# A state-space layer with a mixture of experts: the transposed input of 15 of 16 sequences made by VectorE and DMAs

## The chip, the cores and the metric

The kernel runs on one core of a Trainium2 chip. The metric is the device time of a run in microseconds (us); lower is better. The profile is one further execution, recorded by the hardware. The engines are named as in the profile: PE (TensorE, matmuls; PEld its weight loads), DVE (VectorE), ACT (ScalarE), POOL (GpSimd), SP (SyncE, which here only issues DMAs); SPq and POOLq are the DMA issues of SP and POOL.

## The reference

Sixteen sequences of 256 tokens with 256 features, all in fp32. Both branches take the same layer-normalised input.

```python
xn = layernorm(x)                                   # (16, 256, 256)
# branch 1: selective state space, E=512, N=16, TR=128, K=4
hidden, gate = split(xn @ W_in)                     # 512 + 512 channels
hidden = silu(causal_conv4(hidden) + conv_bias)
dt, Bm, Cm = split(hidden @ W_x, [128, 16, 16])
dts = softplus(dt @ W_dt + b_dt)
state = exp(dts * A) * state + dts * Bm * hidden    # over the 256 tokens, (512, 16)
y = (sum_n(state * Cm) + hidden * D) * silu(gate)
# branch 2: 32 experts of width 96, 8 chosen for each token
w = normalised top 8 of softmax(xn @ router_w.T)
moe = sum_e w[e] * ((silu(xn @ w_gate[e]) * (xn @ w_up[e])) @ w_down[e])
out = x + y @ W_out + moe
```

## The kernel before

**Layout.** Products contract over the 256 features of x, so x is wanted with features on partitions: `xnT_b`, a tile of 128 partitions x 2 x 256 tokens. x comes in with tokens on partitions (`xt`, 128 x 2 x 256) and is normalised there. In branch 1 channels lie on partitions and time runs along the free dimension, where one scan instruction of DVE runs over the tokens.

**Steps.** Each sequence is cut into named steps, which run on one engine each. Ahead of the change: `load_x` (DMA of 256 KB), `stats` (DVE), `root` (ACT), `invert` (DVE), `norm` (ACT, L370), `turn` (PE, four 128x128 transposes into a PSUM bank `pt`, L379), `keep_turned` (ACT, a copy of 128x512 to `xnT_b`, L384). From `xnT_b` start:
- the router: `route` (PE, `pl`, L394), `largest`, `expo`, `choose` (its last instruction is a transpose of 128x64 in blocks of 32x32 on DVE, L432), `send_weights` (four DMAs of 8 KB to the DRAM tile `wd`, L441) and `spread` (six DMAs that spread the weights of eight experts over partitions, `wr`, L457);
- the experts: `gates` (`pg`) and `ups` (`pu`, both L471), `silu` (ACT, `sg`, L484), `weigh` (POOL, L490), `combine` (DVE, `h`, L494), `down` (PE, `acc`, L506), for 12 pairs of 128 columns of the hidden layer;
- the state space: `project` (PE, `ph`, L517), `conv_first` (ACT, L529), `conv_rest` (DVE, L540), `activate` (ACT, L547), `params` (PE, `px`, L555), `keep_params`, `send_params` (DMA of 32 KB to DRAM, `bcd`, L571), `widen` and `steps` (`pdt`, softplus), `inputs` (POOL, L609). Then eight groups of two states: `fetch` (DMA of 512 KB that spreads the rows of B and C over the partitions, `rep`, L618), `feed` (POOL, `bu`, L630), `decay` (ACT, `da`, L644), `scan` (DVE, L652), `read` (DVE, `pr`, L664), `collect` (POOL's DMAs that add into `y`, L669);
- the end of a sequence: `fold`, `gate` (PE, `pgate`, L697), `gate_silu`, `gated` (POOL, L713), `project_out` (PE, `po`, L723), `finish`, `store`.

**What sets the order.** A planner (`Plan`, L20 to L117) lists all steps of all sequences ahead of the build. Each step has an engine, a length, the steps that it needs, the ring slots that it takes and gives back, and a due time. On each engine the ready step with the earliest due time goes first; on ACT a step that needs no other function table counts as due `STAY` earlier; a step isn't ready before due time less `EARLY`. The instructions are then issued in that order, and each engine runs its own list in order. So a step that waits holds back what stands behind it on its engine; that holds for SP's DMAs too. Due times are a base (`ORIGIN`, `PERIOD` a sequence, `RATE` and `LEAD` for the experts) and a table entry for the kind of step (`DUE`, with `FIRST` for sequence 0 and `LAST` for sequence 15).

**Rings.** `xnT` has three slots, `rep` and `bu` three, `pr` four; PSUM has two banks each of kind `g` and `u`, used in turn by `pg`, `pu`, `ph`, `px`, `pdt`, `po` and, of kind `u`, `pt`. The tile `xt` has one slot, so the next x is loaded when this one has been turned.

Of the kernel before, what the change touches and what calls it, by code (L numbers as in the profile page):

```python
# [11 lines left out]
F32 = mybir.dt.float32  # L12
# [7 lines left out]
class Plan:  # L20
# [7 lines left out]
    SWITCH = 1.3  # L28
    HANDOVER = dict(PE=0.27, DVE=0.14, ACT=0.12, POOL=0.1, SP=0.1)
    MARGIN = dict(PE=0.4, DVE=0.1, ACT=0.1, POOL=0.1, SP=0.0)  # L30
    STAY = 8.6

    def __init__(self, rings):
        self.size = rings
# [86 lines left out]
def mamba_moe_kernel(  # L121
# [30 lines left out]
    nc = tc.nc  # L152
    P = 128
    B, L, H = x.shape
# [5 lines left out]
    HC = H // P  # L160
    EC = E // P
    SPS = L // P
# [13 lines left out]
    SPP = SLOTS // PARTS  # L176
    FAR = 1e30
    SLOWEST = 1e-26
    ORIGIN = -8.4
    PERIOD = 79.3  # L180
    RATE = 79.8

    DUE = dict(
        load_x=-120.5, stats=-16.5, root=-64.0, invert=-262.0, norm=218.5, turn=-490.0,
        keep_turned=-136.0, route=-110.0, largest=-337.5, expo=50.5, choose=-1121.5,
        send_weights=-122.5, project=-72.0, conv_first=402.5, conv_rest=236.0, activate=-361.5,
        params=-140.5, keep_params=-203.5, send_params=-258.5, widen=-105.5, steps=-57.0,
        skip=99.0, inputs=-255.0, fetch=-414.5, feed=399.0, decay=-22.0, scan=427.0, read=68.9,
        collect=-162.5, spread=41.0, gates=-37.5, ups=607.5, silu=230.0, weigh=115.0,
        combine=-69.0, down=114.0, settle=-364.0, gate=38.0, gate_silu=-13.0, fold=508.5,  # L190
        gated=598.5, project_out=-129.5, load_again=-28.5, finish=5.5,
    )
    EARLY = dict(
        load_x=169.0, load_experts=25.0, stats=37.0, turn=155.0, route=255.0, project=501.0,
    )

    FIRST = dict(
        route=248.0, largest=4.5, expo=0.5, choose=551.5, project=287.5, conv_first=-504.5,
        conv_rest=-239.5, activate=150.0, params=-457.5, keep_params=163.5, widen=6.0, steps=770.5,
        skip=-277.5, inputs=137.5, fetch=-152.0, feed=-250.0, decay=-61.0, scan=-50.5, read=-70.5,  # L200
        collect=-120.5, spread=-96.0, gates=-48.0, ups=-216.5, silu=-173.5, weigh=271.5,
        combine=239.0, down=-66.5,
    )

    LAST = dict(
        fetch=-293.5, feed=1.0, decay=252.5, scan=589.0, read=109.5, collect=-95.0, spread=0.5,
        gates=198.5, ups=131.0, silu=192.0, weigh=-110.0, combine=538.5, down=189.5, settle=2.5,
        gate=7.5, gate_silu=223.0, fold=-22.5, gated=238.5, project_out=-415.5, finish=519.5,
    )
    LEAD = -29.6  # L210
    TOPK = 8
    EPS = 1e-5

    xf = x.rearrange("b l h -> (b l) h")
# [3 lines left out]
    p1 = ctx.enter_context(tc.tile_pool(name="p1", bufs=1))  # L218
    sb = ctx.enter_context(tc.tile_pool(name="sb", bufs=1))
    ps = ctx.enter_context(tc.tile_pool(name="ps", bufs=1, space=PSUM))  # L220
    dram = ctx.enter_context(tc.tile_pool(name="dram", bufs=3, space=DRAM))

    RINGS = dict(
        sk=1, xt=1, mv=1, st=1, std=1, xnT=3, nmax=1, rest=1, dt=1, hs=2, dts=2, y0=2, y1=2,
        rep=3, bu=3, pr=4, da=AHEAD, g=2, u=2, acc=1, wr=2, sg=3, h=2, gs=2, o=1,
    )
    taken = defaultdict(int)
# [8 lines left out]
    live = {}  # L236
# [129 lines left out]
    def norm(b):  # L366
        xt = live["xt", b]
        rstd, nmr = live.pop(("st", b))
        for s in range(SPS):
            nc.scalar.activation(  # L370
                xt[:, s, :], xt[:, s, :], AF.Identity, bias=nmr[:, s, :], scale=rstd[:, s, :]
            )

    def turn(b):
        xn = live.pop(("xt", b))
# [371 lines left out]
    b = 0  # L747
    MM = 0.432
    KB = 1 / 280

    def add(kind, key, engine, length, due, *args, early=None, **kw):
        fn = kw.pop("fn", None) or steps_of[kind]
        if early is None:
            early = EARLY.get(kind, 1e9)
        due += DUE.get(kind, 0.0) + (FIRST.get(kind, 0.0) if b == 0 else 0.0)
        due += LAST.get(kind, 0.0) if b == B - 1 else 0.0
        plan.add((kind, *key), engine, length, due, fn, *args, early=early, **kw)

    steps_of = dict(
        load_x=load_x, stats=stats, root=root, invert=invert, norm=norm, turn=turn,  # L760
        keep_turned=keep_turned, route=route, largest=largest, expo=expo, choose=choose,
        project=project, conv_first=conv_first, conv_rest=conv_rest, activate=activate,
        params=params, keep_params=keep_params, widen=widen, steps=steps, skip=skip, inputs=inputs,
        fetch=fetch, spread=spread, gates=gates, ups=expand, silu=silu, combine=combine,
        weigh=weigh, down=down, settle=settle, gate=gate, gate_silu=gate_silu, gated=gated,
        project_out=project_out, load_again=load_again, finish=finish, store=store, feed=feed,
        add_skip=add_skip, fold=fold, send_params=send_params, send_weights=send_weights, collect=collect, decay=decay, scan=scan, read=read,
        turn_router=turn_router, keep_router=keep_router, warm=warm, grow=grow, shrink=shrink, load_router=load_router, load_in=load_in,
        load_steps=load_steps, load_out=load_out, load_experts=load_experts,
    )  # L770
# [14 lines left out]
    for b in range(B):  # L785
        t = ORIGIN + PERIOD * b
        last = [] if b else [("load_in", 0)]
        x = ("x", b)
        add("load_x", (b,), "SP", 256 * KB, t if b else -210.0, b, takes=[("xt", x)],
            needs=[("turn", b - 1)] if b else [], lands=11.0 if b else 3.5)  # L790
        add("stats", (b,), "DVE", 0.9, t, b, needs=[("load_x", b)],
            takes=[("mv", ("mv", b)), ("st", ("st", b)), ("std", ("rs", b))], gives=[("st", b)])
# [3 lines left out]
            gives=[("mv", b)])  # L796
        add("norm", (b,), "ACT", 1.09, t, b, needs=[("invert", b)],
            gives=[("rs", b)])
        xT = ("xnT", b)
        add("turn", (b,), "PE", 1.0, t, b, needs=[("norm", b)], gives=[x],  # L800
            takes=[("u", ("pt", b)), ("xnT", xT)])
        add("keep_turned", (b,), "ACT", 0.6, t, b, needs=[("turn", b)],
            gives=[("pt", b)])
        add("route", (b,), "PE", 0.9, t if b else t + 30.0, b, needs=[("keep_turned", b), ("keep_router",)],
            takes=[("g", ("pl", b)), ("nmax", ("nmax", b)), ("rest", ("rest", b))], gives=[xT])
        add("largest", (b,), "DVE", 0.25, t, b, needs=[("route", b)])
# [31 lines left out]
        add("inputs", (b,), "POOL", 2.5, t, b, needs=[("steps", b, 0), ("steps", b, 1),  # L838
            ("params", b)] + [("skip", b, c) for c in range(EC)])
        for g in range(GROUPS):  # L840
            at = t + PERIOD / GROUPS * g
            add("fetch", (b, g), "SP", 512 * KB, at, b, g, needs=[("send_params", b)],
                takes=[("rep", ("rep", b, g))], lands=5.5, early=14.0)

        for r in range(UNITS):
            k = UNITS * b + r
            g, u = divmod(r, PAIRED)
            at = t + PERIOD / UNITS * r
            add("feed", (k,), "POOL", 2.31, at, k, needs=[("fetch", b, g), ("inputs", b)],
                takes=[("bu", ("bu", k))], gives=[hs])  # L850
            for j in range(CPU):
# [27 lines left out]
        for i in range(PAIRS // BATCH):  # L879
            at = e + RATE * BATCH / PAIRS * i  # L880
            qs = range(BATCH * i, BATCH * (i + 1))
            for q in qs:
                part = 2 * q // CPG
                add("ups", (b, q), "PE", 4 * MM, at, b, q, "u", gives=[xT], takes=[("u", ("u", b, q))],
                    needs=[("keep_turned", b)] + ([] if b else [("load_experts", part, "u")]))
                add("weigh", (b, q), "POOL", 1.23, at, b, q, gives=[("wr", b, part)],
                    needs=[("silu", b, i), ("spread", b, part)])
                add("combine", (b, q), "DVE", 0.6, at, b, q,
                    needs=[("weigh", b, q), ("ups", b, q)],
                    takes=[("h", ("h", b, q))], gives=[("u", b, q), ("sg", b, q)])  # L890
                add("down", (b, q), "PE", 4 * MM, at, b, q, gives=[("h", b, q)],
                    needs=[("combine", b, q)] + ([("down", b, q - 1)] if q else [])
# [10 lines left out]
            gives=[("acc", b)])  # L903
# [57 lines left out]
```

## Time and profile before

| | |
|---|---|
| median of 3 runs (lowest to highest) | 1326.89 us (1322.99 to 1330.68) |
| the profiled execution, its own time | 1322.61 us |
| its span, first to last instruction | 1320.8 us |
| granted clock of PE, mean | 0.996 |
| turn: PE transposes / ACT copies | x64, 11.2 us busy / x16, 9.4 us busy |
| ACT table loads for decay / silu (L484) / steps | x148 / x81 / x29, 1283 ns each |
| POOL bu, L630 | x256, 715.5 us busy, 68.2 us idle before it |
| SPq rep waiting for DVE pr | 342.3 us, 79 times |

Busy time is what an instruction group took on its engine; idle before it is time in which the engine had nothing to do until that instruction could start, with the instruction that released it. The time of a run is the span and 1.8 us around it. Waits of SP are often no loss: the queue stands ready until a buffer is free. PE's records are pipelined, so a matmul shown with 381 ns starts about 216 ns after the one ahead of it; what a group costs on PE is read from the starts of its neighbours.

### The profile page before, as it was taken

How to read it: one execution, taken by the hardware profiler on the slowest of the kernel's cores; microseconds unless marked ns; L12 is line 12 of the kernel's file. 1: busy time of each engine (PE TensorE's matmuls, PEld its weight loads, DVE VectorE, ACT ScalarE, POOL GpSimd, SP SyncE). 2: the span in 40 equal slices, each digit the busy share in tenths (PEclk: the TensorE clock that was granted, in tenths of full speed). 3: DMA queues.
4: the chain of work that ended last, by engine and by line, in shares of the span. 5: the costliest groups of instructions: out<-in, count | busy, mean ns of one | idle time of the engine just before them, and what ended most of it. 6: DMA issues, size and time to landing. Idle time of an engine off the chain costs nothing.

```text
span 1320.8 us, 18891 instructions
## 1 busy us (share of the span) xinstructions
PE 1290.6 (98%) x5968; PEld 1108.5 (84%) x5968; DVE 1178.9 (89%) x1735; ACT 1129.6 (86%) x1895; POOL 1184.6 (90%) x803
## 2 busy tenths in 40 slices
PE   8999999999999999999999999999999999999998
PEld 6878888878888887888888888888888888888887
DVE  3688999899989999989999898998989899899986
ACT  5888798888888988899898998989899898988873
POOL 0789899989998998998999999998999989898995
PEclk9999999999999999999999999999999999999999
DMA  9998898898988999999899998999889899998994
GB/s 252 238 254 190 193 212 208 198 210 192 216 187 178 217 219 203 199 197 216 189 216 199 219 204 185 217 198 216 199 194 216 191 205 198 208 205 192 196 222 93
DMA packets 174035, 268.79 MB, mean 204 GB/s; under 512 B 37840, under 2 KB 112112, under 8 KB 173936
## 3 DMA queue, kind: packets, MB, share of 16 engines
q0 software_dynamic: 40672, 124.80, 50.4%
q1 hardware_dynamic: 130624, 142.75, 39.9%
q8 instruction: 47, 0.77, 0.2%
q10 hardware_dynamic: 2640, 0.05, 0.1%
q14 instruction: 52, 0.43, 0.1%
HBM read 137.51 MB, written 5.24 MB: 108 GB/s over the span
## 4 chain that ended last, share of the span: by engine, by line
PE 56%; DVE 13%; POOL 10%; DMA 8%; issue 7%; ACT 5%; SPq 0%; ACTq 0%; POOLq 0%; DVEq 0%
PE pu L471 14%; PE acc L506 14%; PE pg L471 13%; DVE da L652 6%; DMA rep<-bcd 5%; POOL bu L630 4%; PE px L555 4%; DVE pr L664 3%; PE po L723 3%; POOL sg L490 3%; PE ph L517 3%; PE pgate L697 2%; ACT da L644 2%; POOL y L669 2%; PE pdt L578 2%
## 5 line engine op out<-in xcount | busy, mean ns | idle before, releaser
L630 POOL TENSOR_TENSOR bu<-rep,hs 128x1024 f32<-128x1024 f32 x256 | 715.5, 2947 | 68.2 <-DVE da L652 44.2
L652 DVE TENSOR_TENSOR_SCAN da<-da,bu 128x512 f32<-128x512 f32 x512 | 608.2, 1216 | 40.1 <-ACT da L644 36.2
L644 ACT ACTIVATE da<-dts,a_sb 128x256 f32<-128x256 f32 x1024 | 468.9, 473 | 88.2 <-DVE pr L664 64.7
L471 PE MATMUL pu<-xnT,wu_sb 128*128 128x256 f32 x1536 | 361.7, 381 | 9.5 <-DVE h L494 8.6
L506 PE MATMUL acc<-wd_sb,h 128*128 128x256 f32 x1536 | 363.2, 379 | 0.9 <-DVE h L494 0.8
L471 PE MATMUL pg<-xnT,wg_sb 128*128 128x256 f32 x1536 | 349.9, 381 | 4.0 <-ACT sg L484 3.2
L490 POOL TENSOR_TENSOR sg<-sg,wr 128x512 f32<-128x512 f32 x192 | 318.2, 1971 | 34.8 <-ACT sg L484 34.4
L471 PEld LDWEIGHTS pu<-xnT,wu_sb 128*128 128x128 f32 x1536 | 291.3, 191 | 52.3 <-DVE h L494 11.7
L471 PEld LDWEIGHTS pg<-xnT,wg_sb 128*128 128x128 f32 x1536 | 292.4, 191 | 47.0 <-ACT sg L484 5.3
L669 POOL DMA_DIRECT2D y<-pr x222 | 319.8, 1446 | 9.7 <-DVE pr L664 3.7
L506 PEld LDWEIGHTS acc<-wd_sb,h 128*128 128x128 f32 x1536 | 291.2, 190 | 41.3 <-DVE h L494 2.0
L664 DVE TENSOR_TENSOR pr<-da,rep 128x512 f32<-128x512 f32 x448 | 294.2, 677 | 3.4 <-DMA y<-pr 1.6
L644 ACT ACT_TABLE_LOAD x148 | 189.9, 1283 | 2.6
L494 DVE TENSOR_TENSOR h<-pu,sg 128x512 f32<-128x512 f32 x192 | 131.1, 683 | 52.0 <-POOL sg L490 25.3
L484 ACT ACTIVATE sg<-pg 128x512 f32<-128x512 f32 x192 | 105.3, 594 | 8.3 <-PE pg L471 5.5
L484 ACT ACT_TABLE_LOAD x81 | 103.9, 1283 | 3.0 <-PE pg L471 1.6
L540 DVE SCALAR_TENSOR_TENSOR hs<-ph,small,hs 128x255 f32<-128x255 f32 (+2 forms) x192 | 76.1, 471 | 0.0
L713 POOL TENSOR_TENSOR y<-y,gs 128x512 f32<-128x512 f32 x30 | 74.3, 2953 | 0.1
L555 PE MATMUL px<-hs,wx_sb 128*32 128x256 f32 (+1 forms) x256 | 62.8, 393 | 3.0 <-ACT sg L484 3.0
L723 PE MATMUL po<-wout_sb,y 128*128 128x256 f32 x256 | 60.9, 381 | 4.1 <-POOL y L713 3.1
L517 PE MATMUL ph<-xnT,win_sb 128*128 128x256 f32 x256 | 64.3, 397 | 0.0
L688 POOL TENSOR_TENSOR y<-y 128x512 f32<-128x512 f32 x32 | 63.9, 2399 | 0.1
(65 smaller groups left out, 868.5 us busy)
## 6 DMA issues: line engine op xcount, KB each, us to landing
y<-pr POOLq DMA_DIRECT2D x222, 512.0 KB, 7.4
rep<-bcd SPq DMA_DIRECT2D x128, 512.0 KB, 6.1
wr<-wd SPq DMA_DIRECT2D x128, 192.0 KB, 5.4
wr<-wd SPq DMA_DIRECT2D x128, 128.0 KB, 5.5
wr<-wd SPq DMA_DIRECT2D x128, 64.0 KB, 5.3
y<-sk POOLq DMA_DIRECT2D x32, 256.0 KB, 5.9
xt<-L_attn_input_states_dram SPq DMA_DIRECT2D x16, 256.0 KB, 5.7
o<-L_attn_input_states_dram SPq DMA_DIRECT2D x16, 256.0 KB, 6.8
```

The lines of the kernel that those rows point to most:

```text
L471: nc.tensor.matmul(p[:, j, :], w[:, hc, ts(c, P)], xs[:, hc, :], start=(hc == 0), stop=(hc == HC - 1),)
L484: nc.scalar.activation(sg, live.pop(("g", b, q)), AF.Silu)
L490: nc.gpsimd.tensor_mul(sg, sg, wr[:, r : r + 2, :])
L494: nc.vector.tensor_mul(h, live.pop(("u", b, q)), live.pop(("sg", b, q)))
L506: nc.tensor.matmul(acc[:, s, :], h[:, j, ts(s, P)], wd_sb[:, c, :], start=(c == 0 and s == 0), stop=(c == FC - 1), skip_group_check=True,)
L517: nc.tensor.matmul(ph[:, j, :], win_sb[:, hc, ts(2 * q + j, P)], xs[:, hc, :], start=(hc == 0), stop=(hc == HC - 1),)
L555: nc.tensor.matmul(p, w[:, c, :], hs[:, c, :], start=(c == 0), stop=(c == EC - 1))
L630: nc.gpsimd.tensor_mul(bu, live["rep", b, g][:, 0:1].to_broadcast([P, CPU, NG, L]), live["hs", b][:, ts(u, CPU), :].unsqueeze(2).to_broadc ...
L644: nc.scalar.activation(da[:, i, :], dts[:, c, :], AF.Exp, scale=a_sb[:, c, n : n + 1])
L652: nc.vector.tensor_tensor_scan(flat, flat, live["bu", k][:, j].rearrange("p n l -> p (n l)"), 0.0, op0=ALU.mult, op1=ALU.add,)
L664: nc.vector.tensor_mul(live["pr", k][:, j], live.pop(("da", m)), live["rep", b, g][:, 1])
L669: nc.gpsimd.dma_start(live["y", b, u].rearrange("p c n l -> p (c n l)"), live.pop(("pr", k)).rearrange("p c n l -> p (c n l)"), accum_op=A ...
```

## The change

For sequences 1 to 15 the step `turn` moves from PE to DVE: one instruction transposes each 32x32 block of `xt` within itself, into a new tile `xb` (one slot). The blocks are then put in their places by DMAs on SP: `send_x` writes them to a DRAM tile `xd` of 256 features x 256 tokens, in eight DMAs of 32 partitions x 8 x 32 elements (32 KB each, runs of 32 floats), and `keep_turned` reads `xd` back as `xnT_b` in one DMA of 256 KB. Sequence 0 keeps the transposes of PE and the copy of ACT. All constants of the planner's due times change, a table for sequence 1 is added, and `STAY` goes from 8.6 to 16.9. What is computed is the same.

```diff
-    STAY = 8.6
+    STAY = 16.9
...
-    ORIGIN = -8.4
+    ORIGIN = -7.2
     PERIOD = 79.3
-    RATE = 79.8
+    RATE = 79.0
...
     EARLY = dict(
-        load_x=169.0, load_experts=25.0, stats=37.0, turn=155.0, route=255.0, project=501.0,
+        load_x=153.0, load_experts=21.0, stats=37.0, turn=7.0, send_x=91.0, route=363.0,
+        project=463.0,
     )
...
-    LEAD = -29.6
+    LEAD = -39.2
     TOPK = 8
+    TB = 32
...
-        sk=1, xt=1, mv=1, st=1, std=1, xnT=3, nmax=1, rest=1, dt=1, hs=2, dts=2, y0=2, y1=2,
+        sk=1, xt=1, xb=1, mv=1, st=1, std=1, xnT=3, nmax=1, rest=1, dt=1, hs=2, dts=2, y0=2, y1=2,
...
+    def flip(b):
+        xn = live.pop(("xt", b))
+        xb = p1.tile([P, SPS, H], F32, tag="xb", name=f"xb_{b}")
+        nc.vector.transpose(
+            xb.rearrange("p s h -> p (s h)"), xn.rearrange("p s h -> p (s h)")
+        )
+        live["xb", b] = xb
+
+    def send_x(b):
+        xb = live.pop(("xb", b)).rearrange("p s (g t) -> p s g t", t=TB)
+        xd = dram.tile([H, L], F32, tag="xd", name=f"xd_{b}")
+        for q in range(P // TB):
+            for s in range(SPS):
+                nc.sync.dma_start(
+                    xd.rearrange("(g h) (s q t) -> s q h g t", h=TB, s=SPS, t=TB)[s, q],
+                    xb[ts(q, TB), s],
+                )
+        live["xd", b] = xd
+
+    def fetch_x(b):
+        xs = take(sb, "xnT", [P, HC, L], f"xnT_{b}")
+        nc.sync.dma_start(xs, live.pop(("xd", b)).rearrange("(c p) l -> p c l", p=P))
+        live["xnT", b] = xs
...
+        due += SECOND.get(kind, 0.0) if b == 1 else 0.0
...
-        add("turn", (b,), "PE", 1.0, t, b, needs=[("norm", b)], gives=[x],
-            takes=[("u", ("pt", b)), ("xnT", xT)])
-        add("keep_turned", (b,), "ACT", 0.6, t, b, needs=[("turn", b)],
-            gives=[("pt", b)])
+        if b == 0:
+            add("turn", (b,), "PE", 1.0, t, b, needs=[("norm", b)], gives=[x],
+                takes=[("u", ("pt", b)), ("xnT", xT)])
+            add("keep_turned", (b,), "ACT", 0.6, t, b, needs=[("turn", b)],
+                gives=[("pt", b)])
+        else:
+            add("turn", (b,), "DVE", 0.6, t, b, fn=flip, needs=[("norm", b)], gives=[x],
+                takes=[("xb", ("xb", b))])
+            add("send_x", (b,), "SP", 3.4, t, b, needs=[("turn", b)], gives=[("xb", b)], lands=6.0)
+            add("keep_turned", (b,), "SP", 256 * KB, t, b, fn=fetch_x, needs=[("send_x", b)],
+                takes=[("xnT", xT)], lands=6.0)
```

Left out are the new values of `DUE`, `FIRST` and `LAST`, of which nearly all change, and the new table `SECOND` with 44 entries (from -192.0 to 224.0).

More of the change, by code (lines that the diff above doesn't have):

```diff
@@ L178, in mamba_moe_kernel @@
     SLOWEST = 1e-26
-    ORIGIN = -8.4
+    ORIGIN = -7.2
     PERIOD = 79.3
-    RATE = 79.8
+    RATE = 79.0
     DUE = dict(
[L184 to L191, printed above, removed]
+        load_x=-72.5, stats=-15.5, root=-34.5, invert=-76.5, norm=313.5, turn=-598.5,
+        keep_turned=-111.5, route=-118.5, largest=-237.5, expo=87.0, choose=-1192.0,
+        send_weights=-223.5, project=-27.0, conv_first=583.5, conv_rest=131.0, activate=-475.5,
+        params=-116.5, keep_params=-304.5, send_params=-109.0, widen=-214.5, steps=-60.5,
+        skip=-24.0, inputs=-315.5, fetch=-278.0, feed=405.5, decay=-23.0, scan=431.5, read=69.4,
+        collect=-148.5, spread=-13.5, gates=-8.0, ups=707.0, silu=266.0, weigh=215.0,
+        combine=-242.5, down=338.5, settle=-523.5, gate=45.0, gate_silu=-13.0, fold=572.0,
+        gated=595.0, project_out=-2.0, load_again=-46.5, finish=-43.0,
@@ L192, in mamba_moe_kernel @@
     )
     EARLY = dict(
-        load_x=169.0, load_experts=25.0, stats=37.0, turn=155.0, route=255.0, project=501.0,
+        load_x=153.0, load_experts=21.0, stats=37.0, turn=7.0, send_x=91.0, route=363.0,
+        project=463.0,
     )
     FIRST = dict(
-        route=248.0, largest=4.5, expo=0.5, choose=551.5, project=287.5, conv_first=-504.5,
-        conv_rest=-239.5, activate=150.0, params=-457.5, keep_params=163.5, widen=6.0, steps=770.5,
-        skip=-277.5, inputs=137.5, fetch=-152.0, feed=-250.0, decay=-61.0, scan=-50.5, read=-70.5,
@@ L201, in mamba_moe_kernel @@
-        collect=-120.5, spread=-96.0, gates=-48.0, ups=-216.5, silu=-173.5, weigh=271.5,
-        combine=239.0, down=-66.5,
+        route=214.5, largest=-39.0, expo=113.0, choose=475.5, project=260.5, conv_first=-707.0,
+        conv_rest=-293.5, activate=296.0, params=-346.5, keep_params=261.5, widen=23.5,
+        steps=847.0, skip=-301.0, inputs=142.0, fetch=-175.5, feed=-16.5, decay=-38.5, scan=167.5,
+        read=-22.5, collect=-252.0, spread=-144.5, gates=-65.5, ups=-212.0, silu=-128.0,
@@ new lines, in mamba_moe_kernel @@
+        weigh=293.5, combine=226.5, down=-220.5,
+    )
+    SECOND = dict(
+        load_x=-192.0, stats=-103.5, root=-105.5, invert=224.0, norm=-87.5, turn=-135.0,
+        keep_turned=123.0, route=-11.5, largest=-54.0, expo=-82.5, choose=57.5,
+        send_weights=-107.0, project=-25.5, conv_first=-31.5, conv_rest=108.5, activate=-23.5,
+        params=-3.5, keep_params=39.5, send_params=220.5, widen=-95.5, steps=149.0, skip=-20.0,
+        inputs=212.5, fetch=-6.0, feed=-21.5, decay=-94.5, scan=41.5, read=29.5, collect=79.0,
+        spread=-67.0, gates=9.0, ups=-10.0, silu=51.5, weigh=14.0, combine=87.5, down=-21.0,
+        settle=96.5, gate=3.5, gate_silu=167.5, fold=-40.5, gated=91.0, project_out=46.0,
+        load_again=-41.5, finish=190.0,
@@ L203, in mamba_moe_kernel @@
     )
     LAST = dict(
-        fetch=-293.5, feed=1.0, decay=252.5, scan=589.0, read=109.5, collect=-95.0, spread=0.5,
-        gates=198.5, ups=131.0, silu=192.0, weigh=-110.0, combine=538.5, down=189.5, settle=2.5,
-        gate=7.5, gate_silu=223.0, fold=-22.5, gated=238.5, project_out=-415.5, finish=519.5,
+        fetch=-267.0, feed=61.5, decay=327.5, scan=428.0, read=-123.0, collect=-218.0, spread=16.5,
+        gates=123.0, ups=381.5, silu=249.0, weigh=-155.0, combine=676.0, down=153.5, settle=-109.0,
@@ L209, in mamba_moe_kernel @@
+        gate=-57.5, gate_silu=105.0, fold=154.0, gated=126.5, project_out=-437.0, finish=566.5,
     )
-    LEAD = -29.6
+    LEAD = -39.2
     TOPK = 8
+    TB = 32
     EPS = 1e-5
@@ L372, in norm @@
             )
+    def flip(b):
[13 more added lines that the diff above has]
+                    xb[ts(q, TB), s],
+                )
+        live["xd", b] = xd
[3 more added lines that the diff above has]
+        live["xnT", b] = xs
     def turn(b):
@@ L766, in mamba_moe_kernel @@
         project_out=project_out, load_again=load_again, finish=finish, store=store, feed=feed,
-        add_skip=add_skip, fold=fold, send_params=send_params, send_weights=send_weights, collect=collect, decay=decay, scan=scan, read=read,
+        add_skip=add_skip, fold=fold, send_params=send_params, send_x=send_x, send_weights=send_weights, collect=collect, decay=decay, scan=scan, read=read,
         turn_router=turn_router, keep_router=keep_router, warm=warm, grow=grow, shrink=shrink, load_router=load_router, load_in=load_in,
```

## The prediction

> **What bounds the kernel now.** I read first the page's busy shares, then the windows of 80 us, then the chain of waits, then the queue of SP.
>
> ```profile
> span 1320.8 us, 18891 instructions
> PE 1290.6 (98%) x5968; PEld 1108.5 (84%) x5968; DVE 1178.9 (89%) x1735; ACT 1129.6 (86%) x1895; POOL 1184.6 (90%) x803
> ...
> q0 software_dynamic: 40672, 124.80, 50.4%
> q1 hardware_dynamic: 130624, 142.75, 39.9%
> ```
>
> Four engines and the DMAs are all near full; PE is the fullest, with 1320.8 - 1290.6 = 30.2 us idle. Where those lie, the windows tell (length, busy time and instructions of PE, PEld, DVE, ACT, POOL, then clock, DMA share, GB/s):
>
> ```profile
> 240.00:320.00 80.00, 77.59 (x363) 66.69 (x362) 75.81 (x108) 69.03 (x115) 75.27 (x52) 1.00 0.91 199
> 720.00:800.00 80.00, 80.00 (x376) 69.46 (x376) 73.60 (x111) 72.21 (x120) 74.97 (x52) 1.00 0.91 204
> 800.00:880.00 80.00, 80.00 (x376) 69.45 (x376) 73.27 (x109) 72.19 (x121) 74.80 (x51) 1.00 0.93 203
> ```
>
> From about 640 to 1120 us PE never stops; from 160 to 640 us it loses 12.2 us (the six windows there have 77.46, 77.59, 77.23, 80.00, 77.33, 78.24 busy), 2.0 us for each sequence. The chain of waits says what one stretch of PE costs (start, length, what):
>
> ```profile
> 767.79 1.73 PE acc L506 x8
> 769.51 0.44 PE pt L379 x4
> 769.95 1.73 PE pu L471 x8
> 771.68 3.45 PE pgate L697 x16
> ```
>
> The pieces abut: 767.79 + 1.73 is 769.52, where the four transposes start, and 0.44 us later comes the next product. The next pgate of the chain starts at 851.03: one sequence costs 79.35 us, all of it PE. So here time off PE is time off the end, until another engine takes over; DVE has 80 - 73.3 = 6.7 us left in 80, POOL 5.0, ACT 7.8.
>
> A rule of the Trainium skill would read this otherwise. "Perfetto Trace Analysis" (Identifying the Most-Contended Engine) says that matmul busy time misjudges how near PE is to its limit, and wants LDWEIGHTS busy time. Here that is 69.46 of 80, which would leave 10.5 us free, and taking transposes away would bring nothing. But the chain shows instructions that abut, with no release between them; I go by the chain.
>
> **What goes.** Of 16 sequences, 15 lose four transposes on PE: 15 x 0.44 = **6.6 us**. PE's waits for them go too: for the normalised x 2.2 us in all, of which 1.4 belong to sequence 0, which keeps its transposes, so 0.8; and 1.0 for the copy that empties their bank (pu waiting for ACT xnT). Together **1.8 us**. ACT loses 15 copies of 0.59 us (8.8 us), and by the order of its instructions 8 of 308 table switches at 1.283 us (10.3 us): it is not on the chain in the steady stretch, so I count nothing for that.
>
> **What DVE gets.** One transpose of 128x512, which the trace doesn't show. The nearest row is that of the small one (L432):
>
> ```profile
> L432 DVE STREAM_TRANSPOSE wT<-rest 128x64 f32<-128x64 f32 x16 | 3.9, 245 | 0.5
> ```
>
> Two other DVE rows give a slope: a product of 128x64 takes 224 ns (L429), one of 128x512 677 ns (L664), so 1.0 ns per element. 245 + 448 x 1.0 gives 0.70 us; the upper end is eight of the small ones, 1.96 us. I take 0.7, as only the stream grows. Both ends fit in DVE's 6.7 us. Without that cover it would be 15 x 0.7 = 10.5 us.
>
> **What the DMAs get.** Per sequence eight writes of 32 KB in runs of 32 floats (128 B), that is 2,048 packets, and one read of 256 KB in 256 packets of 1 KB. Here a rule speaks against the change: "VectorE: DVE Perf Modes" (The three transpose paths) warns that a plain DMA that transposes by strides is 19 times slower than the crossbar's 1.309 us for 128x128 in bf16. By that rule (an estimate from that page) 256 KB, eight such blocks, would take 8 x 19 x 1.309 = 199 us per sequence, more than twice the period, and the kernel would take some 15 x (199 - 79) = 1,800 us more. But the elements were turned before, inside blocks of 32, and the DMA moves whole runs. The trace has just such a transfer: wd<-wT writes rows of 32 floats into rows of DRAM 1 KB apart.
>
> ```profile
> wd<-wT SPq DMA_DIRECT2D x64, 8.0 KB, 4.2
> rep<-bcd SPq DMA_DIRECT2D x128, 512.0 KB, 6.1
> bcd<-bc SPq DMA_DIRECT2D x16, 32.0 KB, 4.5
> ```
>
> The 4,096 packets of 128 B took 14.8 ns each in the trace's packet records, those of 1 KB on the same queue 55.6 ns. So 2,048 x 14.8 / 16 engines = 1.9 us, and 256 x 55.6 / 16 = 0.9: **2.8 us of DMA time per sequence** on some 73 (0.92 of 79.35). The other end is the mean of all packets of q1 (39.9% of 16 x 1320.8 us over 130,624 packets: 64.6 ns), 8.3 us for the writes. I take the row of like packets. The share isn't a ceiling at 1: it adds packets of both queues that overlap, and stretches of 1 us at 1.2 occur (919 to 920 us). Cover: rep, the only DMA on the chain, has room, as follows.
>
> **What SP gets, and who queues behind.** Eight issues of 0.6 us (median of wd<-wT) are 4.8 us, and the read must wait for the last write to land (4.2 to 4.5 us by the last rows). In the new order of SP the eight stand (but for sequences 1 and 2) between rep_1 and rep_4 of the sequence before; behind them stand a rep, the wr of that quarter, and the next x. In all 15 a rep stands between the writes and the read, so the writes mostly land during a wait that SP has anyway (it waits 342 us for DVE pr in all). How late may a rep be? In the steady stretch rep_0 is issued at 900.26, lands about 6.1 later, and its first feed on POOL starts at 912.96: 6.6 us to spare; for rep_1 (908.81, feed 922.27) 7.4; for rep_2 (917.50, feed 934.73) 11. The 4.8 us are covered. Uncovered, a late rep stops POOL's bu, and behind it DVE's scans and POOL's sg, for which h and then PE wait.
>
> The new path for one x is 0.7 + 4.8 + 4.2 + 5.7 (xt's landing as the row for the read) = 15.4 us, against 0.44 + 0.59 before. In the steady stretch of before the transposes end at 928.5 and route starts at 944.0: 15.5 us, so at the old places this would just do. But the new order has the writes behind rep_1 or rep_2, and the read of most sequences right behind rep_2 or rep_3. In the times of before, rep_3 goes out at 928.5, so xnT would land near 935, 9 us ahead of route. So x comes in time: cost nothing; only in sequence 15, where the read follows rep_4 (937.64 + 5.7 = 943.3), is there no room.
>
> **What moves.** All due times are new, so the order changes everywhere. Two things I can weigh. In the order before, sequences 7 to 12 repeat nearly the same list, the one that keeps PE full; after, hardly two agree. From the gates to the product with their h there lie at least 28 matmuls (12.1 us) in those sequences before, 20 to 24 in sequences 6, 7, 10, 11 and 12 after. And from ph to px, for which convolution and silu took 6.2 us in the trace (791.4 to 797.6), there are 28 matmuls before, 12 (5.2 us) in sequence 2 after: 1.0 us of wait there. In the first 100 us sequence 1's projection goes behind 192 matmuls and transposes in place of 84, so that PE has experts' work where it waited 8.2 us (12 to 130 us). I count these against each other as nothing, with 12 us to the worse (2.0 us of wait in each of the six full sequences as in the earlier ones) and 6 us to the better (half of the 12.2 us).
>
> **Sum.** The profiled run took 1322.6 us (span 1320.8 and 1.8 around it). 1322.6 - 6.6 - 1.8 = 1314.2. The median of the three runs shown is 1326.9, 4.3 above it; the same saving from there gives **1318.5**.
>
> **The rivals.** A measurement of this kernel can tell about 0.5%, 6.6 us, from no change: faster is below 1320.3, slower above 1333.5.
> - *As summed*, 1318.5, its own range 1313 to 1324: chance 0.45. For: the abutting pieces. Against: the gain is just the size of what can be told.
> - *The new order also fills earlier waits*: 6 us more, 1312.5. Chance 0.18. For: 8.2 us of waits near the start, and a bank less in use.
> - *The uneven order brings waits back* in the full stretch: 1318.5 + 12 = 1330.5. Chance 0.22. For: the shorter distances. Against: every other engine has 5 us or more to spare in each sequence, and can catch up.
> - *Slower: SP holds rep back.* If the writes land like the slowest wd (7.9 us) while SP stands at the read, a rep comes 4.8 + 7.9 = 12.7 us late. Beyond 6.6 us POOL's bu starves, 6.1 us, and beyond POOL's spare 79.35 - 74.9 = 4.4 the sequence gets longer: 1.7 x 15 = 25 us, 1344. From a lateness of 11 us on it decides. Against: the rep between. Chance 0.15.
>
> That the change doesn't do what it says is out: the four transposes are gone from PE's order in 15 sequences.
>
> Range 1308 to 1335: it leaves out most of the last rival and the lower edge of the second. Faster: two thirds of the first case and the second, 0.48; slower: the last and a quarter of the third, 0.21; same 0.31.
>
> **What would show it.** Right: pgate to pgate near 78.9 us in a stretch with PE at 80.00 of 80; PE busy near 1284; the transpose at 0.7 us; the writes landing in 4 to 5 us with 15 ns packets; no wait of POOL bu for rep beyond 1,000 us. Wrong: PE below 79 of 80 in windows after 640 us (by h: the order; by pl or ph for xnT: the path of x), bu waiting for rep, or packets of 128 B much slower than 15 ns, with the DMA share at 1 and rep landing late.

## The result, and the profile after

The changed kernel takes **1368.66 us** in the median of four runs (1363.49 to 1375.12), the kernel before 1324.94 beside it: a ratio of 1.0335 (95%: 1.0305 to 1.0365). It is slower, by 44 us; 1318.5 was forecast, so the forecast is 50 us off. The profiled execution took 1363.49 us.

The page of the changed kernel, its span, busy shares and DMA queues:

```profile
span 1361.6 us, 18968 instructions
...
PE 1300.4 (96%) x5908; PEld 1113.5 (82%) x5908; DVE 1195.5 (88%) x1750; ACT 1113.4 (82%) x1872; POOL 1184.1 (87%) x803
...
q0 software_dynamic: 40672, 124.80, 48.9%
q1 hardware_dynamic: 167344, 150.62, 41.6%
```

PE has the 60 matmuls less that were forecast, and is still busy for 9.8 us more. Idle is 1361.6 - 1300.4 = 61.2 us, where it was 30.2. These two parts, 31.0 and 9.8, are the whole growth of the span (40.8 us). The windows of 80 us that stood in the prediction show where (length, busy time and instructions of PE, PEld, DVE, ACT, POOL, then clock, DMA share, GB/s):

```profile
240.00:320.00 80.00, 76.83 (x355) 65.79 (x355) 75.41 (x109) 65.48 (x112) 72.57 (x49) 1.00 0.88 195
...
720.00:800.00 80.00, 76.10 (x347) 65.48 (x347) 69.82 (x106) 66.94 (x114) 69.70 (x49) 0.98 0.89 197
800.00:880.00 80.00, 77.11 (x353) 66.14 (x352) 70.22 (x107) 67.90 (x114) 72.14 (x49) 0.98 0.93 205
```

PE, at 80.00 of 80 from 720 to 880 us before, now pauses there, and does 347 and 353 matmuls instead of 376 in such a window. No other engine has become full: DVE and POOL do less in these windows than before. In the two later ones the clock is 0.98 in place of 1.00. So no engine got more work than it can do; the work seems to come at the wrong times, and the experiments look for the reason.

The new pieces themselves have the prices that were worked out. The view of DMA issues (KB each, median us from issue to landing) and groups of DVE (count, busy us, mean ns, idle before it; the row of L361 is from the kernel before):

```profile
rep<-bcd SPq DMA_DIRECT2D x128, 512.0 KB, 6.7
...
xd<-xb SPq DMA_DIRECT2D x120, 32.0 KB, 5.3
xnT<-xd SPq DMA_DIRECT2D x15, 256.0 KB, 7.1
...
wd<-wT SPq DMA_DIRECT2D x64, 8.0 KB, 4.8
```

```profile
L361 DVE SCALAR_TENSOR_TENSOR nmr<-mv,rstd 128x2 f32<-128x2 f32 x16 | 21.8, 1360 | 0.6
...
L374 DVE SCALAR_TENSOR_TENSOR nmr<-mv,rstd 128x2 f32<-128x2 f32 x16 | 32.0, 1999 | 0.6
...
L703 DVE TENSOR_TENSOR pr<-da,rep 128x512 f32<-128x512 f32 x448 | 293.6, 675 | 1.3
...
L392 DVE STREAM_TRANSPOSE xb<-xt 128x512 f32<-128x512 f32 x15 | 10.3, 688 | 3.8 <-ACT xt L383 3.8
```

The transpose takes 688 ns (forecast 0.70 us), and the packets of 128 B take 14.9 ns each in the packet records (forecast 14.8). But rep lands in 6.7 us instead of 6.1, and an instruction that the change doesn't touch, nmr, a product of two columns, takes 1999 ns in the mean instead of 1360. What stands behind these two is told with the experiments.

**One stall, followed from end to end.** The worst of the windows is 160 to 240 us, with PE at 71.74 of 80 (77.46 before). The chain of waits leads through `221.36 8.56 DMA rep<-bcd`; the timeline, here taken from four engines (start, length, what, and idle time before it with its releaser), shows both ends of it:

```profile
207.43 8.16 SPq L402 DMA_DIRECT2D xd<-xb  x8
215.69 5.03 SPq L496 DMA_DIRECT2D wr<-wd  x6
220.81 0.42 SPq L253 DMA_DIRECT2D xt<-L_attn_input_states_dram  x1
221.36 0.39 SPq L657 DMA_DIRECT2D rep<-bcd  x1
...
230.09 2.33 POOL L669 TENSOR_TENSOR bu<-rep,hs 128x1024 f32<-128x1024 f32 x1 [8.17 <-DMA rep<-bcd]
...
234.91 0.69 DVE L533 TENSOR_TENSOR h<-pu,sg 128x512 f32<-128x512 f32 x1 [7.34 <-POOL sg L529]
...
235.66 3.78 PE L545 MATMUL acc<-wd_sb,h 128*128 128x256 f32 x8 [5.12 <-DVE h L533]
...
241.99 1.89 PE L545 MATMUL acc<-wd_sb,h 128*128 128x256 f32 x8
```

SP issues without a pause from 207.43 to 221.36: the eight writes hold it for 8.2 us, the six wr for 5.0, then x, and only then rep. rep lands 8.56 us later. Its buffer had been free since 215.49, when DVE's last read of it ended, so the queue held this rep for 5.9 us. POOL has stood for 8.17 us for it; behind bu stands POOL's sg, for which DVE's h waits, and for h PE waits 5.12 us. PE pays once more: the eight matmuls after the pause take 3.78 us, where the same eight take 1.89 a little later. That is half the clock: the trace's clock records have 0.50 from 232.67 on, for 6.83 us.

### The profile page after: what moved, and what is told of

It reads as the page before. It is cut to its first block, busy times and chain, and to the rows that moved or that the text cites. A ratio compares the mean times of both kernels' runs of the same rounds, so it can differ in the third digit from the quotient of the medians.

```text
span 1361.6 us, 18968 instructions
## 1 busy us (share of the span) xinstructions
PE 1300.4 (96%) x5908; PEld 1113.5 (82%) x5908; DVE 1195.5 (88%) x1750; ACT 1113.4 (82%) x1872; POOL 1184.1 (87%) x803
## 4 chain that ended last, share of the span: by engine, by line
PE 49%; DVE 12%; POOL 11%; ACT 10%; DMA 9%; issue 8%; SPq 1%; ACTq 0%; POOLq 0%; DVEq 0%
PE acc L545 12%; PE pg L510 11%; PE pu L510 11%; DVE da L691 5%; POOL bu L669 4%; PE px L594 3%; PE po L762 3%; ACT da L683 3%; POOL sg L529 3%; DVE pr L703 3%; PE ph L556 3%; DMA rep<-bcd 3%; PE pgate L736 2%; DMA wr<-wd 2%; DMA xnT<-xd 2%
## 5 line engine op out<-in xcount | busy, mean ns | idle before, releaser
L669 POOL TENSOR_TENSOR bu<-rep,hs 128x1024 f32<-128x1024 f32 x256 | 703.9, 2878 | 90.9 <-DVE da L691 46.2
L545 PE MATMUL acc<-wd_sb,h 128*128 128x256 f32 x1536 | 369.9, 384 | 14.4 <-DVE h L533 14.4
L545 PEld LDWEIGHTS acc<-wd_sb,h 128*128 128x128 f32 x1536 | 295.5, 193 | 58.3 <-DVE h L533 16.2
L708 POOL DMA_DIRECT2D y<-pr x222 | 292.9, 1327 | 27.6 <-DVE pr L703 11.4
L523 ACT ACTIVATE sg<-pg 128x512 f32<-128x512 f32 x192 | 105.2, 594 | 15.9 <-DVE h L533 8.9
L556 PE MATMUL ph<-xnT,win_sb 128*128 128x256 f32 x256 | 67.7, 412 | 0.0
L762 PEld LDWEIGHTS po<-wout_sb,y 128*128 128x128 f32 x256 | 49.3, 195 | 16.4 <-POOL y L752 8.2
## 6 DMA issues: line engine op xcount, KB each, us to landing
wr<-wd SPq DMA_DIRECT2D x128, 192.0 KB, 5.3
```

The source lines that it names most:

```text
L523: nc.scalar.activation(sg, live.pop(("g", b, q)), AF.Silu)
L545: nc.tensor.matmul(acc[:, s, :], h[:, j, ts(s, P)], wd_sb[:, c, :], start=(c == 0 and s == 0), stop=(c == FC - 1), skip_group_check=True,)
L556: nc.tensor.matmul(ph[:, j, :], win_sb[:, hc, ts(2 * q + j, P)], xs[:, hc, :], start=(hc == 0), stop=(hc == HC - 1),)
L669: nc.gpsimd.tensor_mul(bu, live["rep", b, g][:, 0:1].to_broadcast([P, CPU, NG, L]), live["hs", b][:, ts(u, CPU), :].unsqueeze(2).to_broadc ...
L708: nc.gpsimd.dma_start(live["y", b, u].rearrange("p c n l -> p (c n l)"), live.pop(("pr", k)).rearrange("p c n l -> p (c n l)"), accum_op=A ...
L762: nc.tensor.matmul(po[:, s, :], y[:, j, 0, ts(s, P)], wout_sb[:, c, :], start=(c == 0 and s == 0), stop=(c == EC - 1), skip_group_check=True,)
```

## The experiments

Three causes were to be told apart: the **writes** (SP held, packets, a late x), the **order** (all due times new), and **nmr** on DVE. Each time is the median beside runs of the kernel before, with the ratio to it and its 95% interval.

**Order and way crossed.** The first run takes the new due times, but leaves the turn on PE for all sequences except sequence 1, which keeps the new way. The second takes the old due times and the new way of x.

```diff
-        if b == 0:
+        if b != 1:
             add("turn", (b,), "PE", 1.0, t, b, needs=[("norm", b)], gives=[x],
```

> The changed kernel's due times, but sequences 2 to 15 are turned by PE and copied by ACT as before (sequence 1 keeps the DMA way, since without it the planner finds no order with these due times). If the order that the new due times make is what costs (order theory): 1350 to 1370 us, with half-clock stretches of PE as in the changed kernel. If the way of x by DVE, DRAM and SP costs (DMA theory): 1320 to 1330.

> The old due times and STAY, with sequences 1 to 15 turned by DVE and DMAs. Order theory: the old due times keep PE full in the second half, 1315 to 1330 us. DMA theory: 1350 us or more, with PE waiting for xnT and POOL for rep. If any due times have to be tuned for the way of x, this one is the slowest of all, over 1370, and neither theory alone holds.

Measured: 1377.83 us, 1.0391 (1.0361 to 1.0421), and 1393.07 us, 1.0512 (1.0472 to 1.0552). Both mixtures are slower than the kernel before, and the second is slower than the changed one; the first is so by 9 us, but its interval just overlaps. So neither theory holds alone: the new due times are slow without most of the DMAs too, and the new way with the old due times costs more (67 us) than with its own (44). The two runs can't split the loss into parts, as each builds an order of its own.

**Taking the writes away.** The order stays that of the changed kernel, instruction for instruction but for the eight writes. The read takes x itself, so the data are not turned, and what is computed from them isn't the layer.

```diff
-        for q in range(P // TB):
-            for s in range(SPS):
-                nc.sync.dma_start(
...
-        nc.sync.dma_start(xs, live.pop(("xd", b)).rearrange("(c p) l -> p c l", p=P))
+        live.pop(("xd", b))
+        nc.sync.dma_start(xs, xf[ts(b, L), :].rearrange("(c p) h -> p c h", p=P))
```

> The changed kernel's order of steps, but the eight writes of each x to DRAM are left out and the read of 256 KB takes the input x itself from DRAM, so xnT doesn't hold the turned x and the output isn't the reference's. DMA theory: SP is no longer held for 6 to 8 us a sequence and no read waits for writes, so 1320 to 1330 us. Order theory: 1350 to 1365.

Measured: 1340.53 us, 1.012 (1.0089 to 1.0152). This run splits the error: **1368.7 - 1340.5 = 28 us for the eight writes, and 1340.5 - 1318.5 = 22 us for the rest**, which is the new order with DVE's transposes and the read of 256 KB left in. The page and the waits (total us, times, longest) of this run:

```profile
span 1338.4 us, 18799 instructions
```

```profile
POOL bu L664 <- DMA rep<-bcd: 15.9, 11, 2.7
...
PE acc L540 <- DVE h L528: 4.8, 2, 3.9
```

In the changed kernel the same two rows are, with one more, and then POOL's row in the kernel before:

```profile
POOL bu L669 <- DMA rep<-bcd: 28.9, 15, 8.2
...
PE acc L545 <- DVE h L533: 14.4, 7, 5.1
...
PE pl L433 <- DMA xnT<-xd: 8.1, 3, 3.9
```

```profile
POOL bu L630 <- DMA rep<-bcd: 16.1, 11, 3.1
```

So POOL's long waits for rep, and two thirds of the time that acc waits for h, come with the writes; without them POOL waits for rep as in the kernel before. The third row, the router's product waiting for the new x, looked like another cost.

**A late x, packets, or the queue of SP?** One run keeps the writes, but reads x from the input, so that the read need not wait for their landing. A second also cuts each write to one eighth of its packets. In both, xnT isn't the turned x.

```diff
-        nc.sync.dma_start(xs, live.pop(("xd", b)).rearrange("(c p) l -> p c l", p=P))
+        nc.sync.dma_start(xs, xf[ts(b, L), :].rearrange("(c p) h -> p c h", p=P))
...
-                    xd.rearrange("(g h) (s q t) -> s q h g t", h=TB, s=SPS, t=TB)[s, q],
-                    xb[ts(q, TB), s],
+                    xd.rearrange("(g h) (s q t) -> s q h g t", h=TB, s=SPS, t=TB)[s, q][:, 0:1],
+                    xb[ts(q, TB), s][:, 0:1],
```

> The changed kernel with its eight writes, but the read takes the input x from DRAM and so waits for no write (xnT then doesn't hold the turned x). Leaving the writes out together with that wait gave 1340.5 us, 28 less than the changed kernel. If it is the late x (the wait of the read for the writes, and of route for the read): near 1343. If it is what the writes do to SP and to the other DMAs: 1360 or more.

> As the last, with an eighth of each write: 32 packets in place of 256, the same eight issues on SP (xnT doesn't hold the turned x). If SP's time and its waits for free places cost: as the last run within 3 us. If the packets cost (1.9 us of all DMA engines a sequence): nearer to 1340.

Measured: 1368.5 us, 1.032 (1.0288 to 1.0352), and 1353.88 us, 1.0213 (1.0185 to 1.0242). Freeing the read changes nothing. But this run doesn't settle what a late x costs: the read still stands behind the writes on SP, and pl still waits 9.7 us for it. So one more run issued that read, of x itself as before, from ACT's queue:

```diff
-        nc.sync.dma_start(xs, xf[ts(b, L), :].rearrange("(c p) h -> p c h", p=P))
+        nc.scalar.dma_start(xs, xf[ts(b, L), :].rearrange("(c p) h -> p c h", p=P))
```

> The changed kernel with its eight writes on SP, but the read takes the input x from DRAM and is issued by ACT, so it stands behind no write and waits for none (xnT doesn't hold the turned x). In the earlier run with a free read PE still waited 9.7 us for xnT, since the read stood behind the writes on SP. If the late x is what the hold on SP costs: 1345 to 1355. If the hold costs by rep and wr: 1360 to 1370.

Measured: 1370.83 us, 1.0343 (1.0305 to 1.0382). Now pl waits only 1.2 us for xnT, and the time is that of the changed kernel. That speaks against a late x as the main cost, but doesn't rule it out: with the read on its queue ACT lets pl wait 5.7 us for a decay (1.7 in the changed kernel), and POOL waits longer for rep. The rows of the three runs (read freed, fewer packets, read on ACT):

```profile
POOL bu L670 <- DMA rep<-bcd: 26.5, 13, 8.8
```

```profile
POOL bu L670 <- DMA rep<-bcd: 13.5, 12, 2.7
...
PE acc L546 <- DVE h L534: 9.8, 6, 3.5
...
PE pl L434 <- DMA xnT<-L_attn_input_states_dram: 9.2, 3, 3.6
```

```profile
POOL bu L670 <- DMA rep<-bcd: 37.3, 14, 10.0
...
PE pl L434 <- ACT da L684: 5.7, 2, 2.9
```

From the first to the second run seven eighths of the packets go, and 14.6 us with them; POOL's long waits for rep go too. From there to no writes at all it is another 13.4 us (1353.9 - 1340.5), for eight small DMAs that still hold SP. These 13.4 us don't come by way of rep, for which POOL waits no longer than in the run without writes (13.5 and 15.9 us). PE waits longer for h (9.8 against 4.8) and for xnT (9.2 against 3.0); what the hold delays on the way there was not separated, and a late x may be part of it.

From the first issue to the end of the eighth the small writes take 6.5 us in the mean of 15 sequences, and those of the changed kernel 7.5 (5.2 to 11.6), where 4.8 was forecast. Why it is more than eight times a single issue (median 456 ns), the waits of SP's queue in the changed kernel tell only in part:

```profile
SPq L402 <- DMA wr<-wd: 7.7, 11, 2.2
...
SPq L402 <- DMA rep<-bcd: 6.0, 7, 2.1
```

The writes don't read wr or rep; they wait for earlier DMAs on the same queue to land. But the two rows are 13.7 us in 15 sequences, 0.9 of the 7.5 us. Of the rest most lies in the issues themselves: eight take 6.1 us in the mean, and a single one up to 4.68. What draws these out isn't shown.

**Fewer, larger writes.** Four writes of 64 KB with the same packets:

```diff
-            for s in range(SPS):
-                nc.sync.dma_start(
-                    xd.rearrange("(g h) (s q t) -> s q h g t", h=TB, s=SPS, t=TB)[s, q],
-                    xb[ts(q, TB), s],
-                )
+            nc.sync.dma_start(
+                xd.rearrange("(g h) (s q t) -> q h s g t", h=TB, s=SPS, t=TB)[q],
+                xb[ts(q, TB)],
+            )
```

> The changed kernel with four writes of 64 KB in place of eight of 32 KB, the same 2,048 packets of 128 B. If the number of issues holds SP: about half of what an eighth of the packets left (13 us), so 1360 to 1363. If only the packets count: 1366 to 1370.

Measured: 1362.11 us, 1.0281 (1.0252 to 1.031). SP is held 5.3 us in the mean, and the median is 6.6 us lower; the intervals of the ratios overlap by a hair, so the direction is likely and the size uncertain. POOL's wait for rep is longer here than in the changed kernel, so that wait alone doesn't set the time:

```profile
POOL bu L668 <- DMA rep<-bcd: 35.1, 16, 7.0
```

**The writes on another queue.** If SP's hold is the cost, ACT might issue the writes:

```diff
-                nc.sync.dma_start(
+                nc.scalar.dma_start(
```

> The changed kernel with its eight writes issued by ACT in place of SP, all else equal. Packets stay, SP's hold (7.5 us a sequence in the profile) goes, ACT gets it, with some 10 us to spare in 80. If the hold on SP is the larger part of the 28 us: 1345 to 1352. If the packets are: 1358 to 1368. If ACT can't bear the hold in the middle of its exponentials: over 1370.

> The changed kernel with both the writes issued by ACT and nmr made by ACT. If the two parts add to what the moved nmr alone brought (1354): 1335 to 1345; if ACT's hold makes up for it: 1354 or more.

Measured: 1466.25 us, 1.1075 (1.1039 to 1.1111); and with the edit of nmr below on top 1455.81 us, 1.0976 (1.0939 to 1.1013). POOL's wait for rep falls to 9.9 us, as it should, but the hold has only moved:

```profile
ACT da L683 <- DMA xd<-xb: 46.0, 5, 15.4
ACT L683 <- DMA xd<-xb: 41.7, 5, 10.7
```

The decays don't read xd: between the two ends of such a wait ACT does nothing but issue the eight writes (510.89 to 517.39 us in one case). Meanwhile it owes decays to DVE, which waits 145.5 us for them, where it was 31.0 in the changed kernel. SP was the better place: it has time between its issues.

**The small instruction on DVE.** In the changed kernel nmr (-mean x rstd, 128x2) once takes 7.57 us. What POOL does in that time (timelines of DVE, POOL and PE):

```profile
524.97 7.57 DVE L374 SCALAR_TENSOR_TENSOR nmr<-mv,rstd 128x2 f32<-128x2 f32 x1
532.46 1.27 DVE L703 TENSOR_TENSOR pr<-da,rep 128x512 f32<-128x512 f32 x2
...
524.23 2.63 POOL L669 TENSOR_TENSOR bu<-rep,hs 128x1024 f32<-128x1024 f32 x1
526.53 1.17 POOL L708 DMA_DIRECT2D y<-pr  x1
527.14 2.94 POOL L669 TENSOR_TENSOR bu<-rep,hs 128x1024 f32<-128x1024 f32 x1
529.45 3.06 POOL L529 TENSOR_TENSOR sg<-sg,wr 128x512 f32<-128x512 f32 x2
...
534.39 3.78 PE L545 MATMUL acc<-wd_sb,h 128*128 128x256 f32 x8 [3.85 <-DVE h L533]
```

nmr ends when POOL's row of products ends (529.45 + 3.06 = 532.51), DVE does nothing else meanwhile, and PE waits 3.85 us for the h behind it. The Trainium skill, "SBUF — State Buffer" (SBUF: two separate sides), says that VectorE and GpSimd share a pair of ports, which one instruction holds alone until it ends, and names a DVE operation with two SBUF inputs as one that needs it. The trace agrees only in part. All eight uses of nmr above 1 us in the changed kernel ended within 0.1 us of the end of a POOL instruction. But the longest outlasts several of them, and the products pr, which have two SBUF inputs as well, don't wait: 303 of the 448 began and ended within a tensor instruction of POOL, and none took more than 0.69 us. So what sets nmr apart isn't shown. The next test can show what nmr costs on DVE, not that the ports hold it. It gives the product to ACT, as three small instructions:

```diff
+        nc.scalar.activation(negm, live["mv", b][:, :, 0:1], AF.Copy, scale=-1.0)
...
-        nc.vector.scalar_tensor_tensor(
-            nmr, mv[:, :, 0:1], -1.0, rstd, op0=ALU.mult, op1=ALU.mult
-        )
...
+        for s in range(SPS):
+            nc.scalar.activation(nmr[:, s, :], negm[:, s, :], AF.Copy, scale=rstd[:, s, :])
```

It was made in the changed kernel, in the one without writes, and in the kernel before.

> The changed kernel with one instruction moved: the product of mean and 1/std (nmr, 128x2, two operands in SBUF), which took 0.16 to 7.57 us on DVE and 33 us in 16, is made by ACT in three small instructions. Port theory (DVE stands still in it while POOL works, PE then waits for h and drops to half clock): DVE gets 30 us back and 4 of the 10 long gaps of PE go with their half-clock stretches, 1335 to 1350 us. If it is only a symptom: 1360 to 1370.

> The changed kernel without the writes and without the read's wait (xnT doesn't hold the turned x), and with nmr made by ACT. Both causes add (28 and 14.5 us): 1326. If what is left of the order costs nothing then, PE is full and 6.6 us less busy than before: 1318. If the two overlap (the same gaps): 1335 or more.

> The kernel before, with nmr made by ACT. Its nmr took 21.8 us on DVE, five times 1.6 to 4.7 us between 269 and 680 us, where PE lost 12 us. Port theory: 1312 to 1320 us, faster than both kernels. If PE's waits there have other causes: 1322 to 1328.

Measured: 1354.18 us, 1.0219 (1.019 to 1.0248); 1337.24 us, 1.0089 (1.0065 to 1.0113); and **1316.86 us, 0.9937 (0.991 to 0.9965)**. That is 14.5 us off the changed kernel; 3.3 us without the writes, where the intervals overlap; and 8.7 us off the kernel before (1325.59 beside it), which makes it **the fastest kernel of this study**. Its page and windows:

```profile
span 1312.9 us, 18943 instructions
...
PE 1286.0 (98%) x5968; PEld 1107.9 (84%) x5968; DVE 1158.1 (88%) x1719; ACT 1135.2 (86%) x1943; POOL 1183.7 (90%) x803
```

```profile
240.00:320.00 80.00, 80.00 (x377) 69.48 (x376) 74.16 (x111) 72.11 (x123) 77.36 (x53) 1.00 0.94 205
...
720.00:800.00 80.00, 80.00 (x377) 69.48 (x376) 72.87 (x109) 72.50 (x124) 75.18 (x52) 1.00 0.91 204
```

The window from 240 us, which lost 2.4 us of PE before, is full. DVE's busy time is 20.8 us less than before (1178.9 - 1158.1), about the 21.8 us that nmr took there. In the changed kernel the 32.0 us of nmr are part of the loss, but it was not the change that put them there: the kernel before pays them too. So nmr adds no third share: with it on ACT the writes cost 17 us (1354.2 - 1337.2) and not 28, so 11 of the 28 come only where nmr is on DVE. The 22 us of the rest don't shrink by it, as the kernel before gains more from the move than the one without writes.

**One constant of the planner alone.** Does any new order cost, or just this one? In the kernel before, with nothing of the new way of x, one constant was given the new value.

```diff
-    STAY = 8.6
+    STAY = 16.9
```

> The kernel before with one planner constant of the changed one, STAY 16.9 for 8.6, and nothing else: no work is added or taken away, only the order moves. Order theory (any order that its due times weren't set for leaves PE gaps and half-clock stretches): 1340 us or more. If only the DMA way made the due times unfit: 1320 to 1332.

```diff
-    ORIGIN = -8.4
+    ORIGIN = -7.2
```

> The kernel before with another of the changed kernel's constants, ORIGIN -7.2 for -8.4: all due times of the state space come 1.2 us later against those of the experts, no work is added. Order theory: any order that the due times weren't set for costs, so 1340 us or more, as with STAY. If STAY was a special case: 1320 to 1330.

Measured: 1375.88 us, 1.0381 (1.0344 to 1.0418), and 1363.41 us, 1.0284 (1.0243 to 1.0325). PE, DVE and POOL have as many instructions as before, and ACT within five. The windows of the run with the new STAY:

```profile
720.00:800.00 80.00, 78.60 (x367) 67.33 (x366) 71.71 (x109) 67.67 (x114) 73.94 (x52) 1.00 0.87 195
800.00:880.00 80.00, 75.60 (x346) 64.47 (x345) 65.08 (x100) 63.75 (x109) 64.47 (x45) 0.98 0.81 179
```

All five engines and the DMAs do less at once: a picture of work that arrives late, as in the changed kernel. So the order of the kernel before is easily lost: two constants, each moved alone to its new value, cost 51 and 39 us, more than the 22 us by which the whole new set misses the forecast without its writes. Other values were not tried.

## Why the prediction was wrong

- **"PE is the bound": right.** The 40.8 us are PE's gaps and PE's clock; no other engine got fuller.
- **What goes, 6.6 us and 1.8 us: right in kind, drowned.** PE has 60 matmuls less. Its busy time should have fallen to 1284; it rose to 1300.4, 16.4 us above, and that is the clock. In the trace's clock records the stretches at half clock add up to 13.5 us before (4 stretches) and 49.0 us after (13). PE was at work in 9.6 and in 42.5 us of them; half of the difference is 16.4. The Trainium skill has a rule, "TensorE: Matmul & The Clock Gate" (Part 1): after PE has been idle for a window of about 3.4 us the clock is halved. The rows agree as to the halving (after waits of 3.85 and 5.12 us eight matmuls took 3.78 us) and the window (the stretches during the kernel last 3.41 or 6.83 us), but not as to the wait: of the twelve that lie within the changed kernel nine came with waits of only 1.6 to 3.3 us. **No step of the sum priced a wait twice**, once as idle time and once as slow matmuls behind it.
- **DVE, 0.70 us: right in length**, 0.688. That it is covered was not tested alone.
- **The DMAs, "2.8 us of DMA time" and nothing for it: the size was right, the zero wrong.** 14.9 ns a packet confirms the choice of the like row over the mean of all packets and over the rule that speaks of 19 times. But 7/8 of the packets were worth 14.6 us of time, more than half of their own 25 us of DMA time (15 x 2,048 x 7/8 x 14.9 ns / 16). With the packets in place rep lands later (median 6.7 us, 6.1 before), and the cover named for it, "rep ... has room", was misread.
- **"How late may a rep be? ... 6.6 us to spare": misread, and "the 4.8 us are covered" with it.** Each rep feeds two bu, and the prediction took the second for the first. The trace of before has, for rep_1:

```profile
908.81 0.45 SPq L618 DMA_DIRECT2D rep<-bcd  x1
...
916.90 2.35 POOL L630 TENSOR_TENSOR bu<-rep,hs 128x1024 f32<-128x1024 f32 x1 [0.48 <-DVE da L652]
...
922.27 2.36 POOL L630 TENSOR_TENSOR bu<-rep,hs 128x1024 f32<-128x1024 f32 x1 [1.96 <-DVE da L652]
```

This rep landed at 915.95, so the room was 1.0 us, not 7.4; for rep_0 (landed 905.77, feed 906.96) it was 1.2 and not 6.6, and for rep_2 (928.42, 928.58) 0.2 and not 11. From 640 to 1120 us the median room is 2.4 us. And the hold was not 4.8 but 7.5 us in the mean and up to 11.6; in the stretch shown six wr between the writes and the rep add 5.0. Eight small writes on SP were worth 13.4 us, yet without longer waits for rep, so the way of these 13.4 us stays open. The rival on the slower side named a late rep, and its 25 us are close to the 28 of all the writes. That is luck: it took the same 6.6 us of room, and its trigger, the read waiting for the writes to land, is not the cause, as freeing the read changed nothing.
- **"x comes in time: cost nothing": wrong as to waiting; the cost is open.** pl waited 8.1 us for xnT in three places. With 1.2 us of that wait left the time was the same, but ACT then paid for the read.
- **"I count these against each other as nothing, with 12 us to the worse": wrong, 22 us.** With the nothing put for the writes (28 us) this is the step that failed; the two make the 50 us. It weighed some distances between instructions that had got longer and some that had got shorter. It did not ask how far the order of before stood from an arbitrary one. One constant alone costs 39 to 51 us; and the new order was made together with the new way of x, which the crossed runs show. Which of the shorter distances makes the 22 us was not separated and stays open.

The sum as the runs give it: 1318.5 + 22 (the rest, without writes) + 13.4 (eight small writes on SP) + 14.6 (packets) = 1368.5, measured 1368.7. The parts are differences from one run to the next, so the sum closes by itself; it doesn't show that they would come out the same in another order.

## What to carry to other kernels

When all engines are nearly full, as here, and one list per engine fixes the order, price a change by what it puts in front of others on an in-order queue, and not by its own busy time. Take the room of a transfer from its first reader. A wait of PE that lowers its clock is paid up to twice: one of 1.58 us (pl, at 88.74 us of the changed kernel) was followed by 3.41 us of matmuls at half clock, 1.7 us more. And look for short instructions with long mean times before moving large ones: moving the 128x2 product gave about as much (8.7 us) as removing the transposes was forecast to give (8.4).

## What the runs showed of the hardware

- A 128x2 product on DVE with two operands in SBUF took from 0.16 to 7.57 us, and in the longest case ended with a series of POOL instructions rather than with the next one. The transposes of 128x512 stayed at 0.69 us in the mean, and so did products of 128x512 with two operands in SBUF, within POOL's instructions too.
- PE's clock was halved for 3.41 or 6.83 us at a time, after waits as short as 1.58 us.
- A burst of eight small DMAs on one queue took 7.5 us to issue, though one issue has a median of 0.46 us, and cutting the packets to one eighth still left 6.5 us. On ACT's queue the same burst cost nearly 100 us more than on SP's (1466.3 against 1368.7).
- Packets of 128 B written to DRAM in rows 1 KB apart cost 14.9 ns each of a DMA engine's time, and 14.6 of the 25 us that seven eighths of them made up came back in the kernel's time, at a DMA share of 0.9.
